# Layer 1's last five groups of tiles as routed pairs instead of dense experts

## The chip, the cores and the metric

The kernel runs on one core of one Trainium2 chip. Its metric is the device time of one execution in microseconds, the median of several runs. The engines are named as in the profile: PE multiplies matrices (PEld loads its weights), DVE works on vectors, ACT on activations and copies, POOL issues the indirect DMAs, and SP issues nearly all the others. Each engine takes its instructions in order, so one that waits holds up everything behind it on that engine.

## The reference

The input `x` has 8192 rows (128 graphs of 64 nodes) of 256 channels in fp32. Two layers follow each other. Each is a graph part over dense 64 x 64 adjacencies, added to `x`, and then a mixture-of-experts FFN over the rows, added to `x` again. The change is in the FFN of layer 1. It has four experts, of which every row uses two:

```python
h = (x_flat @ W_gat).reshape(M, HEADS, NUM_EXPERTS)          # M = B*N nodes of the graph, 4 heads
...   # attention over 1048576 random edges of 65536 nodes gives agg
scores = _layernorm(agg, ln_gamma, ln_beta).reshape(M, HEADS, NUM_EXPERTS).mean(1)
topk_s, topk_i = jax.lax.top_k(scores, TOP_K)                # TOP_K = 2
w = jax.nn.softmax(topk_s, axis=-1)
for ei in range(NUM_EXPERTS):
    g = jnp.where(topk_i == ei, w, 0.0).sum(-1)
    hh = jax.nn.gelu(x @ W1[ei] + b1[ei], approximate=False)  # 256 -> 512
    out = out + g[..., None] * (hh @ W2[ei] + b2[ei])         # 512 -> 256
```

The FFN of layer 1 is fed the layer-normed rows `z` (8192 of them). The weights of a row's two experts (its gates) depend on the attention over the edges and are known late; the outputs of the four experts depend on `z` alone.

## The kernel before

The 8192 rows are 64 tiles of 128 rows (`NT`), in 16 groups of `GR` = 4 tiles (`NG`). `x` stays in SBUF. Layer 0 ends at about 1200 us. In layer 1 there are four stages, and the dense expert work is dealt out over three of them, because it needs no gate to begin.

**The experts of one group** are the generator `experts` (L1025). For each of the four experts it issues four steps `h` (two 128x512 matmuls `ph` at L1035, the gelu at L1039) and four steps `y` (four 128x256 matmuls `py` at L1045, the bias add `y` on DVE at L1049, then `take`). It yields after each of these 32 units, so that the caller can put other work between them. The transposed rows `zT` of a group are loaded from the DRAM copy `zts` by `prepare`, one group ahead. What `take` does depends on the stage. Where the gates are unknown, `keep` stores the output tile to `ystore` (128 KB a time); with gates known, `add` (L1739) does `x += gate * y` on DVE (L1740) and sends the finished tile out (L1742).

**Beside stage, to 1687.5 us.** The graph part of layer 1 goes over the groups in steps: `first`, `second`, `combine`, `tables`. `combine` ends a group's `x`; `tables` (L1198) scales its rows to `z`, transposes them, stores them to `zts`, and makes the edge tables. `filler` (L1233) mixes into these steps the dense units of the first `BESIDE` = 4 groups; its outputs have names `p`, `pw` and `yin`. At the end of the stage the fillers that are left run out.

**Edge stage, to 2202.9 us.** It does the attention over the edges. `prologue` sets up sums, `edges_of_lists` (L1470) then makes 144 indirect gathers on POOL (`got`, L1485), selections on DVE and small matmuls. One of their steps is taken after each dense unit of groups 4 to 10 (`range(BESIDE, EARLY)`). 7 groups are 224 units. At its end is a branch on `n_trips`, the number of blocks of edges that didn't fit the lists; it isn't taken with these inputs.

**Gate stage and the rest.** `gates` (L1652) makes the gates of all 64 tiles, spread over the `y` units of group 11 (`EARLY`), whose outputs are kept too. Groups 12 to 15 then run with `add`. After each second unit the loads and adds of one of the 48 kept tiles are issued: `yin` from `ystore` (512 KB, pool `f2`, 3 buffers), four adds, one output store.

The buffers around the change: PSUM has 4 in the pool `psf`, which `ph` and `py` take from; outputs `y` have 6, gelu outputs `hT` 8.

Of the kernel before, what the change touches and what calls it, by code (L numbers as in the profile page):

```python
# [9 lines left out]
F32 = mybir.dt.float32  # L10
I32 = mybir.dt.int32
# [9 lines left out]
P = 128  # L21
NT = 64
# [41 lines left out]
PL = 24  # L64
NPC = 3
RK = 8
BESIDE = 4
EARLY = BESIDE + 7
HK = 8


# [5 lines left out]
def kernel(  # L77
# [52 lines left out]
        return t  # L130

    const = ctx.enter_context(tc.tile_pool(name="const", bufs=1, reuse_waits="tile"))
    small = ctx.enter_context(tc.tile_pool(name="small", bufs=2, reuse_waits="tile"))


    x = const.tile([P, NT, D], F32, name="x")
# [6 lines left out]
    V.memset(ones_col, 1.0)  # L143
    ones_row = const.tile([1, P], F32, name="ones_row")
    V.memset(ones_row, 1.0)

    def rsqrt(dst, v):

        V.tensor_copy(dst, v)
        s = small.tile([P, NT], F32, name="rs_s")  # L150
        S.activation(s, dst, AF.Sqrt)
        y = small.tile([P, NT], F32, name="rs_y")
        V.reciprocal(y, s)
        w = small.tile([P, NT], F32, name="rs_w")
        V.tensor_tensor(w, y, y, ALU.mult)
        V.tensor_tensor(w, w, dst, ALU.mult)
        V.tensor_scalar(w, w, -0.5, 1.5, ALU.mult, ALU.add)
        V.tensor_tensor(dst, y, w, ALU.mult)

    def root_of_bits(dst, v, guess, work):  # L160

# [847 lines left out]
    def scaled(dst, src, g, norm, k):  # L1009
        scale, shift, mean = factors(g, norm, k)  # L1010
        if norm == 0:
            S.activation(dst, src, AF.Identity, bias=shift, scale=scale)
        else:
            V.tensor_scalar(dst, src, mean, scale, ALU.subtract, ALU.mult)

    zts = dram.tile([NG, P, 2 * GR * P], F32, name="zts")
    ystore = dram.tile([EARLY + 1, GR, P, NEXP * D], F32, name="ystore")
    zTs = {}

    def prepare(g, to):  # L1020
# [3 lines left out]

    def experts(g, to, take, ahead=True):  # L1025

        if ahead and g + 1 < NG:
            prepare(g + 1, to)
        zT = zTs.pop(g)
        for e in range(NEXP):  # L1030
            hTs = []
            for q in range(NH1):
                ph = to["ph"]()
                for c in range(2):
                    nc.tensor.matmul(  # L1035
                        ph, w1[:, e, c, q * P : q * P + P], zT[:, c, :], start=(c == 0), stop=(c == 1)
                    )
                hT = to["hT"]()
                S.activation(hT, ph, AF.Gelu, bias=b1[:, e, q : q + 1])  # L1039
                hTs.append(hT)  # L1040
                yield "h"
            for k in range(GR):
                py = to["py"]()
                for q in range(NH1):
                    nc.tensor.matmul(  # L1045
                        py, hTs[q][:, k * P : k * P + P], w2[:, e, q, :], start=(q == 0), stop=(q == NH1 - 1)
                    )
                y = to["y"]()
                V.tensor_tensor(y, py, b2[:, e * D : e * D + D], ALU.add)  # L1049
                take(e, k, y)  # L1050
                yield "y"
# [7 lines left out]
    with ExitStack() as of_c:  # L1059
# [39 lines left out]
        def transposed(g, norm):  # L1099

            z = cz.tile([P, GR, D], F32, name="z")
            for k in range(GR):
                scaled(z[:, k, :], x[:, GR * g + k, :], g, norm, k)
            yield
            zT = c2.tile([P, 2, GR * P], F32, name="zT")
            for c in range(2):
                tz = psc.tile([P, GR * P], F32, name="tz")
                for k in range(GR):
                    nc.tensor.transpose(tz[:, k * P : k * P + P], z[:, k, c * P : c * P + P], ident)
                S.copy(zT[:, c, :], tz)  # L1110
            return zT
# [85 lines left out]

        def tables(g):  # L1198
            zT = yield from transposed(g, 2)
            nc.sync.dma_start(zts[g], zT.rearrange("p c n -> p (c n)"))  # L1200
            yield
            hps = psc.tile([P, D + 1], F32, name="ph")
            for k in range(GR):
# [353 lines left out]
    with tc.tile_pool(name="em", bufs=2, reuse_waits="tile") as emp, tc.tile_pool(name="pse", bufs=4, space=PSUM, reuse_waits="tile") as pse, tc.tile_pool(  # L1557
# [12 lines left out]
        V.tensor_reduce(some[0:1, :], trips[0:1, 0:P], AX.X, ALU.max)  # L1570
        V.tensor_scalar(n_trips, some[0:1, :], float(n_left), None, ALU.mult)
        n_trips = nc.values_load(n_trips[0:1, 0:1], min_val=0, max_val=n_left)
        for g in range(BESIDE, EARLY):
            for unit in experts(g, to, keep(g)):
                if not over:
                    over = next(steps, 1) == 1
                else:
                    next(edge_steps, None)
        for _ in edge_steps:
            pass  # L1580

# [59 lines left out]
    with tc.tile_pool(name="gp", bufs=1, reuse_waits="tile") as gp, tc.tile_pool(name="f2", bufs=3, reuse_waits="tile") as f2, tc.tile_pool(  # L1641
        name="psf", bufs=4, space=PSUM
    ) as psf:
        def by_channel(v):
            return v.unsqueeze(2).to_broadcast([P, HC, NT])

        def by_node(v, n):
            return v.unsqueeze(1).to_broadcast([P, n, NT])

        gate = gp.tile([P, NEXP, NT], F32, name="gate")  # L1650

        def gates():  # L1652

            agg = gp.tile([P, HC, NT], F32, name="agg")
            V.reciprocal(acc[:, 0:HEADS, :], acc[:, 0:HEADS, :])
            yield
            V.tensor_tensor(
                agg.rearrange("p (h c) t -> p h c t", c=NEXP),  # L1660
                acc[:, HEADS:CH, :].rearrange("p (h c) t -> p h c t", c=NEXP),
                acc[:, 0:HEADS, :].unsqueeze(2).to_broadcast([P, HEADS, NEXP, NT]),
                ALU.mult,
            )
            yield

            V.tensor_tensor(agg, agg, by_channel(bgat), ALU.add)
            yield
            m = gp.tile([P, NT], F32, name="m")
            V.tensor_reduce(m, agg.rearrange("p a t -> p t a"), AX.X, ALU.add)  # L1670
            yield
            V.tensor_scalar(m, m, 1.0 / HC, None, ALU.mult)
            yield
            V.tensor_tensor(agg, agg, by_node(m, HC), ALU.subtract)
            yield
            sq = gp.tile([P, HC, NT], F32, name="sq")
            V.tensor_tensor(sq, agg, agg, ALU.mult)
            yield
            V.tensor_reduce(m, sq.rearrange("p a t -> p t a"), AX.X, ALU.add)
            yield  # L1680
            V.tensor_scalar(m, m, 1.0 / HC, EPS, ALU.mult, ALU.add)
            yield
            rs = gp.tile([P, NT], F32, name="rs")
            rsqrt(rs, m)
            yield
            V.tensor_tensor(agg, agg, by_node(rs, HC), ALU.mult)
            yield
# [1 line left out]
            yield  # L1689
            V.tensor_tensor(agg, agg, by_channel(lnb), ALU.add)  # L1690
            yield
            sc = gp.tile([P, NEXP, NT], F32, name="sc")
            V.tensor_reduce(sc, agg.rearrange("p (h c) t -> p c t h", c=NEXP), AX.X, ALU.add)  # L1693
            yield
            V.tensor_scalar(sc, sc, 1.0 / HEADS, None, ALU.mult)
            yield

            rank = gp.tile([P, NEXP, NT], F32, name="rank")
            V.memset(rank, 0.0)
            yield  # L1700
            for e in range(NEXP):
                for f in range(e + 1, NEXP):
                    ge = f2.tile([P, NT], F32, name="ge")
                    V.tensor_tensor(ge, sc[:, e, :], sc[:, f, :], ALU.is_ge)  # L1704
                    yield
                    V.tensor_tensor(rank[:, f, :], rank[:, f, :], ge, ALU.add)  # L1706
                    yield
                    V.tensor_scalar(ge, ge, -1.0, 1.0, ALU.mult, ALU.add)  # L1708
                    yield
                    V.tensor_tensor(rank[:, e, :], rank[:, e, :], ge, ALU.add)  # L1710
                    yield
            V.tensor_reduce(m, sc.rearrange("p e t -> p t e"), AX.X, ALU.max)
            yield
            V.tensor_tensor(gate, sc, by_node(m, NEXP), ALU.subtract)
            yield
            S.activation(gate, gate, AF.Exp)
            yield
            V.tensor_scalar(rank, rank, 1.5, None, ALU.is_lt)
            yield
            V.tensor_tensor(gate, gate, rank, ALU.mult)  # L1720
            yield
            V.tensor_reduce(m, gate.rearrange("p e t -> p t e"), AX.X, ALU.add)  # L1722
            yield
            V.reciprocal(m, m)  # L1724
            yield
            V.tensor_tensor(gate, gate, by_node(m, NEXP), ALU.mult)
            yield

        steps = gates()

        to = places(psf, psf)
        for unit in experts(EARLY, to, keep(EARLY)):
            if unit == "y":
                for _ in range(4):
                    next(steps, None)
        for _ in steps:
            pass

# [2 lines left out]
            if e == NEXP - 1:  # L1741
                nc.sync.dma_start(out_t[:, t, :], x[:, t, :])  # L1742

        kept = iter([(g, k) for g in range(EARLY + 1) for k in range(GR)])
        for g in range(EARLY + 1, NG):
            n = 0
            for unit in experts(g, to, lambda e, k, y: add(GR * g + k, e, y)):
                n += 1
                if n % 2 == 0:
                    g0, k = next(kept, (None, None))  # L1750
                    if g0 is not None:
                        y = f2.tile([P, NEXP * D], F32, name="yin")
                        nc.sync.dma_start(y, ystore[g0, k])
                        for e in range(NEXP):
                            add(GR * g0 + k, e, y[:, e * D : e * D + D])


# [54 lines left out]
```

## Time and profile before

| | us |
|---|---|
| runs: lowest, median, highest | 2498.76, 2503.37, 2503.64 |
| profiled execution, own time | 2489.01 |
| its span, first to last instruction | 2487.3 |
| beside stage ends; edge stage ends | 1687.5; 2202.9 |
| busy PE, DVE, ACT, POOL (share of the span) | 91%, 63%, 37%, 12% |

The page gives busy times, slices of a fortieth of the span (62.2 us each), and groups of instructions with their mean duration. Matmuls are pipelined, so durations of matmuls are also read as the distance of their starts. The granted TensorE clock has a mean of 0.962. The stages' limits are read from the trace by the first and last instruction of each stage's lines.

### The profile page before, as it was taken

The page shows a single profiled execution, that of the slowest core. Times are in us where ns is not written, and L with a number is a line of the kernel's source. Part 1 is how long each engine was busy: PE and PEld are TensorE (multiplying, and loading weights), DVE is VectorE, ACT ScalarE, POOL GpSimd, SP SyncE. Part 2 cuts the span into 40 slices and gives each one's busy share as a digit, 9 for nine tenths or more (in the row PEclk, how much of TensorE's full clock was granted, in tenths as well). Part 3 has the DMA queues.
Part 4 walks back from the last instruction along what each step waited for, and adds up shares of the span by engine and source line. Part 5 has one row for each costly group of instructions (what it writes and reads, how often), then busy time and mean ns, then how long its engine had stood idle before and what let it go on. Part 6 is the DMA issues. An engine that isn't in the chain of part 4 may idle for free. (4 is left out here: it accounts for less than half of the span.)

```text
span 2487.3 us, 30612 instructions
## 1 busy us (share of the span) xinstructions
PE 2260.3 (91%) x10334; PEld 1441.9 (58%) x10334; DVE 1577.0 (63%) x4448; ACT 931.6 (37%) x1607; POOL 303.8 (12%) x331
## 2 busy tenths in 40 slices
PE   6889998897999999999487999998999999999999
PEld 4444444334566566566355676665676666666666
DVE  7989888317888888883388644615555552157822
ACT  3767666652211211211166757322333232121121
POOL 2011111111000000000331100002344341000000
PEclk9999999998999999999788999999999999999999
DMA  7121112302111121112214111122222121128800
GB/s 212 42 62 45 58 50 77 109 21 71 35 52 45 37 52 45 35 49 64 66 49 134 54 61 46 68 70 47 53 58 50 45 53 45 47 74 264 253 21 15
DMA packets 159204, 170.13 MB, mean 68 GB/s; under 512 B 43312, under 2 KB 137136, under 8 KB 159040
## 3 DMA queue, kind: packets, MB, share of 16 engines
q1 hardware_dynamic: 130848, 145.84, 19.3%
q0 software_dynamic: 10912, 18.31, 3.0%
q10 hardware_dynamic: 17280, 3.93, 0.7%
q8 instruction: 86, 1.41, 0.2%
q14 instruction: 78, 0.64, 0.1%
HBM read 100.42 MB, written 67.60 MB: 68 GB/s over the span
## 5 line engine op out<-in xcount | busy, mean ns | idle before, releaser
L476 PE MATMUL ph<-zT,w 128*128 128x512 f32 x1056 | 528.5, 633 | 32.3 <-ACT hT L479 19.7
L1045 PE MATMUL py<-w,hT 128*128 128x256 f32 x1536 | 362.3, 390 | 21.2 <-ACT hT L1039 12.5
L1035 PE MATMUL ph<-zT,w 128*128 128x512 f32 x768 | 348.3, 600 | 4.6 <-issue 4.2
L1045 PEld LDWEIGHTS py<-w,hT 128*128 128x128 f32 x1536 | 292.4, 194 | 85.8 <-issue 20.4
L476 PEld LDWEIGHTS ph<-zT,w 128*128 128x128 f32 x1056 | 196.7, 200 | 240.6 <-issue 178.7
L479 ACT ACTIVATE hT<-ph,b 128x512 f32<-128x512 f32 x264 | 179.9, 685 | 267.0 <-PE ph L476 264.3
L1039 ACT ACTIVATE hT<-ph,b 128x512 f32<-128x512 f32 x192 | 129.8, 687 | 364.9 <-PE ph L1035 361.6
L305 DVE TENSOR_TENSOR one<-iota_l,pb 128x1024 bf16<-128x1024 bf16 x208 | 253.4, 1218 | 18.0 <-PE cnt_ps L316 18.0
L903 PE MATMUL py<-wd,hT 128*128 x1088 | 250.1, 384 | 0.0
L1049 DVE TENSOR_TENSOR y<-py,b 128x256 f32<-128x256 f32 x192 | 80.8, 422 | 249.4 <-PE py L1045 244.2
L1035 PEld LDWEIGHTS ph<-zT,w 128*128 128x128 f32 x768 | 143.7, 191 | 154.5 <-issue 151.7
L903 PEld LDWEIGHTS py<-wd,hT 128*128 128x128 f32 x1088 | 202.1, 190 | 26.3 <-issue 1.4
L1485 POOL DMA_INDIRECT got<-tsrc,esrc x144 | 153.2, 1064 | 339.3 <-DVE lt L1461 149.7
L1089 POOL DMA_INDIRECT yin<-yrows,row_y x64 | 63.8, 997 | 764.3 <-SPq L966 632.1
L305 DVE TENSOR_TENSOR one<-iota_h,pb 128x512 bf16<-128x512 bf16 x208 | 141.8, 684 | 0.0
L467 ACT COPY zT<-tz 128x256 f32<-128x256 f32 x68 | 23.8, 374 | 291.1 <-PE tz L466 291.1
L622 PE MATMUL pre<-wd 128*128 128x512 f32 x256 | 127.3, 614 | 1.6 <-DVE x L647 0.9
L316 PEld LDWEIGHTS <-one 128*128 128x128 bf16 x1664 | 74.7, 98 | 84.1 <-issue 60.4
L1045 PE MATMUL pw<-w,hT 128*128 128x256 f32 x512 | 118.8, 380 | 0.0
L1035 PE MATMUL p<-zT,w 128*128 128x512 f32 x256 | 117.2, 600 | 1.8 <-ACT hT L1039 1.6
L1045 PEld LDWEIGHTS pw<-w,hT 128*128 128x128 f32 x512 | 94.9, 190 | 18.6 <-issue 6.7
L1740 DVE SCALAR_TENSOR_TENSOR x<-yin,gate,x 128x256 f32<-128x256 f32 x192 | 89.7, 481 | 23.3 <-DMA yin<-ystore 20.1
(369 smaller groups left out, 2999.8 us busy)
## 6 DMA issues: line engine op xcount, KB each, us to landing
yin<-ystore SPq DMA_DIRECT2D x48, 512.0 KB
ystore<-y SPq DMA_DIRECT2D x128, 128.0 KB
zin<-zrows SPq DMA_DIRECT2D x68, 128.0 KB
bd<-in_L_ffn_bd_dram SPq DMA_DIRECT2D x68, 128.0 KB
yrows<-y SPq DMA_DIRECT2D x68, 128.0 KB
x<-in_x_dram SPq DMA_DIRECT2D x8, 1024.0 KB
wd<-in_L_ffn_Wd_dram SPq DMA_DIRECT2D x8, 1024.0 KB
zts<-zT SPq DMA_DIRECT2D x16, 512.0 KB
```

Source lines behind the costliest of these rows:

```text
L305: V.tensor_tensor(o, wi.unsqueeze(1).to_broadcast([P, HK, n]), pb[:, g : g + HK].unsqueeze(2).to_broadcast([P, HK, n]), ALU.is_equal,)
L316: nc.tensor.matmul(self.ps, one[0][:, k, :], one[1][:, k, :], start=(at + k == 0), stop=(at + k == n_chunks * KEPT - 1),)
L476: nc.tensor.matmul(ph, w1[:, c, q * P : q * P + P], zT[:, c, :], start=(c == 0), stop=(c == 1))
L479: S.activation(hT, ph, AF.Gelu, bias=b1[:, q : q + 1])
L622: nc.tensor.matmul(pre, xnT[:, c, n * P : n * P + P], wcat[:, c, :], start=(c == 0), stop=(c == 1),)
L903: nc.tensor.matmul(py, hTs[q][:, k * P : k * P + P], wd[:, bass.ds(ex[k], 1), q, :].rearrange("p e f -> p (e f)"), start=(q == 0), stop=(q ...
L1035: nc.tensor.matmul(ph, w1[:, e, c, q * P : q * P + P], zT[:, c, :], start=(c == 0), stop=(c == 1))
L1039: S.activation(hT, ph, AF.Gelu, bias=b1[:, e, q : q + 1])
L1045: nc.tensor.matmul(py, hTs[q][:, k * P : k * P + P], w2[:, e, q, :], start=(q == 0), stop=(q == NH1 - 1))
L1049: V.tensor_tensor(y, py, b2[:, e * D : e * D + D], ALU.add)
L1485: nc.gpsimd.indirect_dma_start(got, None, tsrc, bass.IndirectOffsetOnAxis(ap=esrc[:, b, at : at + 1], axis=0))
L1740: V.scalar_tensor_tensor(x[:, t, :], y, gate[:, e, t : t + 1], x[:, t, :], ALU.mult, ALU.add)
```

## The change

Layer 1's last five groups (20 tiles of 128 rows, tiles 44 to 63) are no longer computed for all four experts. The other 11 groups (`DENSE`) stay dense. Their distribution is new: 2 groups as fillers (before 4), 5 in the edge stage (before 7), 2 in the gate stage (before 1), and 2 at the very end (before 4).

- **In the tables**, the rows `z` of the routed groups are stored to `zns`, and no `zts` for them.
- **At the start of the edge stage**, 23 DMAs of 256 KB fill the DRAM array `zslots` with zeros. A tile of it has the 128 slots of some rows of one expert. Two steps of the edge work are taken per dense unit before the gathers and behind them, one while they run.
- **In the gate stage**, two steps per unit of groups 7 and 8: gates of the 20 routed tiles first, then `route`, then gates of the other 44. `gates` is written with fewer yields, and its reciprocal square root is made on DVE by `root_of_bits` instead of with ACT's square root. `route` counts by small matmuls how many rows come before each row in its expert, and gives every row two slots (`place`), rounded up to pairs of tiles per expert: 23 pairs at most (`PAIRS`). It loads the `z` rows of five groups (into the `f2` buffers of `yin`) and sends each tile twice to `zslots`, by 40 indirect DMAs on POOL. `pair_e` holds the expert of each pair.
- **`pairs`** goes over the 23 pairs with the expert's number in registers of SP and PE. Each loads its slots, the expert's `w1` (512 KB), `b1` and `b2` from DRAM, transposes, and does the two layers with 128x256 matmuls (`w2` from SBUF at a dynamic place), and stores its two tiles to `yslots`. After each sixth unit a kept tile may be taken.
- **`back`**, beside the dense groups 9 and 10: for each routed tile, two indirect gathers from `yslots`, two adds with `weight`, and its output store.

The diff, cut to its core (the steps of the gates that only lose a yield, and a few lines of set-up, are left out):

```diff
-BESIDE = 4
-EARLY = BESIDE + 7
+BESIDE, EDGES, GATES = 2, 7, 9
+ROUTED = 5
+DENSE = NG - ROUTED
+RT = ROUTED * GR
+PAIRS = RT + 3
...
+            if norm == 2 and g >= DENSE:
+                nc.sync.dma_start(zns[g - DENSE], z.rearrange("p k f -> p (k f)"))
...
-            nc.sync.dma_start(zts[g], zT.rearrange("p c n -> p (c n)"))
+            if g < DENSE:
+                nc.sync.dma_start(zts[g], zT.rearrange("p c n -> p (c n)"))
...
-        for g in range(BESIDE, EARLY):
+        none = e1.tile([P, D], F32, name="none")
+        nc.gpsimd.memset(none, 0.0)
+        for i in range(PAIRS):
+            nc.sync.dma_start(
+                zslots[2 * P * i : 2 * P * i + 2 * P].rearrange("(k p) f -> p k f", p=P),
+                none.unsqueeze(1).to_broadcast([P, 2, D]),
+            )
+        taken = 0
+        for g in range(BESIDE, EDGES):
             for unit in experts(g, to, keep(g)):
-                if not over:
-                    over = next(steps, 1) == 1
-                else:
-                    next(edge_steps, None)
+                for _ in range(1 if over and taken < ET * NB else 2):
+                    if not over:
+                        over = next(steps, 1) == 1
+                    else:
+                        next(edge_steps, None)
+                        taken += 1
...
+        def route():
...
+            for k in range(ROUTED):
+                z = f2.tile([P, NEXP * D], F32, name="yin").rearrange("p (k f) -> p k f", f=D)
+                nc.sync.dma_start(z.rearrange("p k f -> p (k f)"), zns[k])
+                for i in range(GR):
+                    for j in range(2):
+                        t = k * GR + i
+                        send = nc.gpsimd.indirect_dma_start(
+                            zslots, bass.IndirectOffsetOnAxis(ap=place[:, j, t : t + 1], axis=0), z[:, i, :], None
+                        )
+                        for other in sends:
+                            tc.declare_no_dep(send.ins, other, reason="no two write the same row")
+                        sends.append(send.ins)
...
-        for unit in experts(EARLY, to, keep(EARLY)):
-            if unit == "y":
-                for _ in range(4):
-                    next(steps, None)
+        steps = chain(gates(T0, NT), route(), gates(0, T0))
+        for g in range(EDGES, GATES):
+            for unit in experts(g, to, keep(g)):
+                next(steps, None)
+                next(steps, None)
...
+        def kept():
+            for t in range(GATES * GR):
+                y = f2.tile([P, NEXP * D], F32, name="yin")
+                nc.sync.dma_start(y, ystore[t // GR, t % GR])
+                for e in range(NEXP):
+                    add(t, e, y[:, e * D : e * D + D])
+                yield
+
+        def pairs():
+            for i in range(PAIRS):
...
+                e = bass.ds(ex[i % GR], 1)
+                z = fp.tile([P, 2, D], F32, name="zin")
+                nc.sync.dma_start(z, zslots[2 * P * i : 2 * P * i + 2 * P].rearrange("(k p) f -> p k f", p=P))
+                w1e = fp.tile([P, 2, F1], F32, name="w1e")
+                nc.sync.dma_start(w1e, f1_w1[e].rearrange("e (c p) f -> p (e c) f", p=P))
...
+                b2e = fp.tile([P, D], F32, name="b2e")
+                nc.sync.dma_start(b2e, f1_b2[e, :].to_broadcast([P, D]))
+                tz = to["ph"]()
+                for c in range(2):
+                    for k in range(2):
+                        at = (2 * c + k) * P
+                        nc.tensor.transpose(tz[:, at : at + P], z[:, k, c * P : c * P + P], ident)
+                zT = fp.tile([P, 2, 2 * P], F32, name="zTp")
+                S.copy(zT.rearrange("p c n -> p (c n)"), tz)
+                yield
+                hTs = []
+                for q in range(NH1):
+                    ph = to["ph"]()[:, 0 : 2 * P]
...
+                for k in range(2):
+                    py = to["py"]()
...
+                    y = to["y"]()
+                    V.tensor_tensor(y, py, b2e, ALU.add)
+                    nc.sync.dma_start(yslots[(2 * i + k) * P : (2 * i + k + 1) * P, :], y)
+                    yield
+
+        def back():
+            for t in range(RT):
+                ys = []
+                for j in range(2):
+                    y = fb.tile([P, D], F32, name=f"yb{j}")
+                    nc.gpsimd.indirect_dma_start(
+                        y, None, yslots, bass.IndirectOffsetOnAxis(ap=place[:, j, t : t + 1], axis=0)
+                    )
+                    ys.append(y)
+                    yield
+                xs = x[:, T0 + t, :]
+                for j in range(2):
+                    V.scalar_tensor_tensor(xs, ys[j], weight[:, j, t : t + 1], xs, ALU.mult, ALU.add)
+                nc.sync.dma_start(out_t[:, T0 + t, :], xs)
+
+        stored = kept()
+        with tc.tile_pool(name="fp", bufs=2, reuse_waits="tile") as fp:
+            for n, _ in enumerate(pairs()):
+                if n % 6 == 5:
+                    next(stored, None)
+        with tc.tile_pool(name="fb", bufs=3, reuse_waits="tile") as fb:
+            steps = back()
+            for g in range(GATES, DENSE):
+                for n, _ in enumerate(experts(g, to, lambda e, k, y: add(GR * g + k, e, y))):
+                    next(steps, None)
+                    if n % 3 == 2:
+                        next(stored, None)
+            for of in (stored, steps):
+                for _ in of:
+                    pass
```

The tiles are scheduled by the framework, which may issue an instruction ahead of others that stand before it in the code; the order named in the prediction is that of the engines' built instruction streams.

## The prediction

> **What bounds the kernel now.** I read the page's sums and slices first, to see which engine is full and when; then a table of windows, cut where one stage ends; then the groups of instructions in the stages that the change touches; last the chain that ended last, which is matmuls alone from 2351.8 us on. The page:
>
> ```profile
> PE 2260.3 (91%) x10334; PEld 1441.9 (58%) x10334; DVE 1577.0 (63%) x4448; ACT 931.6 (37%) x1607; POOL 303.8 (12%) x331
> ...
> PE   6889998897999999999487999998999999999999
> ...
> DVE  7989888317888888883388644615555552157822
> ```
>
> PE has nine tenths or more in all slices from 1366 us on but one, so what the change takes from PE there is time, unless something else is late. The windows (columns: length; busy PE, PEld, DVE, ACT, POOL with counts; granted clock; DMA share; GB/s):
>
> ```profile
> 1366.00:1560.00 194.00, 190.97 (x877) 134.17 (x876) 106.52 (x348) 128.34 (x208) 8.40 (x8) 1.00 0.16 52
> 1560.00:1600.00 40.00, 40.00 (x177) 28.18 (x176) 35.63 (x150) 15.49 (x24) 0.33 (x2) 1.00 0.26 88
> 1600.00:1640.00 40.00, 40.00 (x172) 28.27 (x172) 4.89 (x14) 8.80 (x14) 0.00 (x0) 1.00 0.21 73
> 1640.00:1688.00 48.00, 47.81 (x187) 33.01 (x186) 7.82 (x21) 9.32 (x14) 0.00 (x0) 1.00 0.19 61
> 1688.00:1720.00 32.00, 31.11 (x128) 19.94 (x129) 25.49 (x67) 9.04 (x12) 1.12 (x2) 1.00 0.26 42
> 1720.00:1800.00 80.00, 70.27 (x350) 47.65 (x349) 39.96 (x96) 24.49 (x61) 36.89 (x35) 0.91 0.22 48
> 1800.00:2060.00 260.00, 250.34 (x1343) 176.53 (x1341) 141.17 (x363) 83.37 (x190) 114.07 (x107) 0.98 0.21 51
> 2202.00:2300.00 98.00, 97.11 (x327) 63.17 (x328) 79.35 (x183) 26.13 (x35) 0.00 (x0) 0.97 0.61 195
> ```
>
> From 1560 to 1688 DVE is nearly done by 1600, and PE works on fillers alone. The edge stage (1687.5 to 2202.9) and the gate stage with the groups behind it (to 2487.3) are full of the same dense expert work. Its groups between 2202 and 2400 us (busy, mean ns of one | idle before):
>
> ```profile
> L1035 PE MATMUL ph<-zT,w 128*128 128x512 f32 x224 | 101.2, 606 | 4.2 <-issue 4.2
> L1045 PE MATMUL py<-w,hT 128*128 128x256 f32 x447 | 99.3, 380 | 1.1 <-DVE y L1049 1.1
> L1740 DVE SCALAR_TENSOR_TENSOR x<-yin,gate,x 128x256 f32<-128x256 f32 x192 | 89.7, 481 | 23.3 <-DMA yin<-ystore 20.1
> ```
>
> The records are pipelined; start to start, a 128x512 matmul takes 0.853 us here and a 128x256 one 0.433. One expert of a group is 8 x 0.853 + 16 x 0.433 = 13.8 us, a group of four tiles 55.1. The third row is the 48 kept tiles: DVE and their loads run beside PE, 48 in 128 us, 2.67 us each, a load landing 4.4 us (median) after its issue. On POOL, from the page, one indirect DMA is:
>
> ```profile
> L1485 POOL DMA_INDIRECT got<-tsrc,esrc x144 | 153.2, 1064 | 339.3 <-DVE lt L1461 149.7
> L1089 POOL DMA_INDIRECT yin<-yrows,row_y x64 | 63.8, 997 | 764.3 <-SPq L966 632.1
> ```
>
> Issued back to back they start 1.28 us apart.
>
> **The change, part by part.** All times are of the profiled execution: span 2487.3, own time 2489.0. That is 14 us (0.6%) under the median of the runs, 2503.4; I add the same 14 us at the end. About 0.2%, 5 us, is what a measurement of this kernel tells from no change.
>
> *Fillers 4 to 2 groups.* Up to 1560 nothing differs. From there groups 2 and 3 are missing: 110.3 us of PE work. But DVE has 35.6 of 40 us until 1600, and the last factors come at 1599; the four last tables follow each other at filler pace (1600, 1620, 1640, 1660) only because fillers lie between them, and need 9 us of PE in all. So the stage ends at about 1602 (1598 to 1612) instead of 1687.5: 85 of the 110 us are gained, 25 are work that was free.
>
> *Edge stage, 7 to 5 groups.* 514.9 less two groups, 404.6 us, if the edge steps are still spread over the units. They are: two steps a unit in the prologue and after the 144th gather, so 160 units suffice; one step a unit between keeps the gathers at their present pace. New there: 23 zero fills of 256 KB, 16 of them on SP's queue ahead of the prologue's loads: 16 x 0.4 us of issue, and 5.9 MB at the 253 to 264 GB/s of the fullest slices is 23 us of transfers; the first gather comes 31 us after the stage's start and PE has units to do, so I put 2 on it (0 to 17). Each of the five routed groups' z rows is stored where zT was, 512 KB for 512 KB: even. Gate stage starts at 1602 + 405 + 2 = 2009 (2000 to 2030), 194 earlier.
>
> *Gates and routing, beside groups 7 and 8.* PE has 2 x 55.1 = 110.3 us of work and three small matmul groups of routing. The gate chain for 20 tiles and the routing go in two steps a unit of 1.72 us: about 38 steps, 33 us until the places are known (25 to 40; the 64-tile chain of before takes 30 at two to four steps a unit; one ACT table load of L151, 1.28 us, goes). Then 40 sends x 1.28 = 51 us on POOL, last landing 87 us in (no indirect send stands in this stage of the trace; the first layer's, L750, and L1485 are the nearest rows: 40 x 1.0 at the least, 40 x 1.3 at the most). Behind them SP's queue is in order: the five z loads share the three kept-tile buffers, so the fourth waits for send 8, the fifth for 16, the first kept tile for 24. Stores of groups 7 and 8 are queued behind those loads; six y buffers fill, and PE stands some 18 us, later 6. The scheduler has put 24 kept loads on SP and 106 kept adds (26 tiles) on DVE ahead of what the first pair needs: pair 0's weights and its bias add. Most of these tiles come after 87 us, at 2.67 us each (lower end 4 adds x 0.48 = 1.95 us; upper end 3.3, if the 4.4 us landing is covered by two buffers only). 87 + 22 x 2.67 = 146, and the first weights, 512 KB loads that landed in 5.5 to 9.7 us when they were first loaded, with four transposes make 156 (140 to 172). PE's 110 us leave 42 of idle time: the moved kept tiles, cheap beside dense groups, are on the path here.
>
> *Pairs for 5 dense groups.* A pair of slots: 4 transposes 0.44, the wait for ACT's copy of 128x512 (0.58, with hand-overs 1.0), 8 + 8 matmuls of 128x256 = 6.94: 8.4 us. 23 of them 193 us, and 4 for six loads of expert numbers into PE's registers (0.6 us each, as the one for n_trips); the 5 groups were 275.7. Saved: 79. The bias adds, gelus and 46 stores of 128 KB lie beside PE: DVE has 2 x 0.42 and ten kept tiles 19 us in 193. Loads of one pair are 0.9 MB, two buffers deep, so they have about 8 us to land; at 195 GB/s, as in the gate stage now, they need 4.6. Hidden; without cover each us counts 23 times.
>
> *Last two groups and the gathers back.* 110.3 us. The 40 gathers need every pair's store and then run at 1.28 us; 32 of them are queued, with their adds, on DVE ahead of the second expert's first bias adds in group 9. They take 41 us plus 3 of landing, PE has some 28 us until it needs those adds: a stall of 15 (8 to 22). Tail as now, 4.
>
> *Clock.* After PE idles the granted clock falls: 0.91 over 80 us in the row from 1720 is 14 us at half rate, 7 lost after one such gap. Four stalls of 6 to 42 us here; I take 8 us for all (4 to 20).
>
> The Trainium skill ("TensorE: Matmul & The Clock Gate", Part 1) has the array at half clock after one idle window of about 3.4 us, until one busy window has passed. By that rule four stalls would cost 4 x 1.7 = 7 us, an estimate; the row says 7 for one, and the sum would be up to 20 higher by it.
>
> Sum: 2009 + 156 + 197 + 110 + 15 + 4 + 8 = 2499 span, 2501 own time, 12 over 2489: **2515 us** on the scale of the median. As a balance: PE's work falls by 79; against it stand 25 us of lost cover, 42 + 15 + 8 of standing and some 6 of zeros and routing, less 5 that the gate stage stood before.
>
> **The rivals.**
> *PE work alone decides (faster).* If kept tiles, sends and gathers hide, the 42, 15 and most of the 8 us are gone: 2515 - 60 = 2455. For it: PE is bound by work everywhere now, and L1740 hides today. Against: 22 kept tiles x 2.67 us cannot lie beside the 23 us of PE work that are left 87 us in. It wins over the forecast if the kept tiles start before the sends finish. Chance 0.20, band 2440 to 2478.
> *A pair waits for its own loads (slower).* Zeros, 512 KB of weights and a broadcast bias land later than 8 us after their issue: the bias broadcast bd of the first layer took 3.9, but first weight loads of 512 KB took 5.5 to 9.7 us. At 10.5 us a pair: 23 x 2.1 = 48 more, 2563. It decides from a landing of 8.4 us on. Against: the DMA share in these stretches is 0.2. Chance 0.18.
> *The stage before does not shrink (slower).* Tables stay 10 to 20 us apart without fillers because their own chain (scale, transpose, copy, matmul, copy, store) is that long: 40 us more, 2555. For: all of it is serial; against: four tables have 13 us of DVE work between 1600 and 1688. Chance 0.07.
>
> **How the numbers follow.** The forecast's case has 0.55, with its own range 2488 to 2540; in it 0.11 is faster, 0.12 within 0.2%, 0.32 slower. Faster 0.20 + 0.11 = 0.31, same 0.12, slower 0.32 + 0.18 + 0.07 = 0.57. For 8 in 10 I leave out the lower half of the first rival (0.10) and the upper half of the second (0.09): 2460 to 2563.
>
> **What would show it.** Right: PE idle from 1560 on with the edge stage at about 1602; gate stage at about 2009; ph of the first pair some 156 us later, waiting on kept adds or its weights; pairs 8.4 us apart, waiting on ACT's zTp; a PE wait in group 9 for DVE. Wrong: pairs further apart than 9 us with DMA as releaser (second rival); no PE gap over 10 us before the pairs (first rival); the edge stage after 1620 (third).

## The result and the profile after

The changed kernel takes 2533.99 us (median of 4 runs, 2530.37 to 2544.07) where the kernel before takes 2503.51 (4 runs): 1.013 of it, 95% interval 1.0096 to 1.0163, 30 us slower. The profiled execution took 2534.8 us, span 2533.1. In the page, busy times and slices (40 of 63.3 us):

```profile
PE 2193.6 (87%) x10206; PEld 1428.8 (56%) x10206; DVE 1556.9 (61%) x4458; ACT 937.8 (37%) x1644; POOL 375.3 (15%) x421
...
PE   6889988897999999999388998789998985799969
...
PEclk9999999997999999999688999699999997899989
```

PE has 67 us less to do than before and stands 87% busy instead of 91%. Where it stands is seen in the slices: 8 7 8 from 1520 to 1710 us, with a clock of 0.6 in the second of them; 8 5 7 from 2026 to 2216 us, in the gate stage; and the 6 from 2406 us on. The windows cut at the stages (length; busy PE, PEld, DVE, ACT, POOL; granted clock; DMA share; GB/s):

```profile
1560.00:1600.00 40.00, 26.00 (x121) 20.60 (x121) 32.30 (x120) 12.24 (x21) 0.64 (x3) 0.68 0.25 85
1600.00:1620.00 20.00, 16.96 (x67) 13.89 (x67) 10.11 (x64) 2.15 (x4) 0.00 (x0) 0.50 0.44 145
2033.00:2100.00 67.00, 53.37 (x168) 32.00 (x168) 38.44 (x148) 16.43 (x21) 24.61 (x26) 0.88 0.31 106
2100.00:2183.00 83.00, 64.66 (x224) 43.77 (x224) 45.40 (x103) 12.39 (x19) 14.31 (x15) 0.86 0.76 243
2183.00:2392.00 209.00, 178.74 (x829) 151.78 (x830) 46.53 (x108) 56.99 (x115) 0.00 (x0) 0.96 0.57 175
2392.00:2450.00 58.00, 34.63 (x108) 21.28 (x107) 24.26 (x56) 5.17 (x8) 38.34 (x40) 0.83 0.47 134
```

Who ended PE's idle time from 2033 us on (us in total, times, longest):

```profile
PE py L1040 <- ACT hT L1034: 47.2, 5, 13.1
PE ph L1899 <- ACT zTp L1893: 16.0, 22, 0.7
PE ph L1899 <- DMA w1e<-in_L_ffn_W_dram: 14.3, 1, 14.3
PE py L1040 <- issue: 7.7, 1, 7.7
```

The first row is put down to ACT, which was not short of time: it had 16, 12 and 5 us of work in the windows from 2033, 2100 and 2392 us. 22.5 of its 47.2 us, and the 7.7, lie between 2086 and 2120 us, beside the sends; 24.7 lie at 2411 and 2440, beside the gathers. PE waits there for gelus that start late. The chain that ended last has them like this beside the sends (start, length, what; the last four gelus are those of one expert):

```profile
2072.86 1.26 ACT hT L1034 x2
2074.13 13.69 another core or an unknown queue
2087.90 0.69 ACT hT L1034
2088.59 7.68 another core or an unknown queue
2096.35 0.69 ACT hT L1034
2097.03 11.13 another core or an unknown queue
2108.25 0.69 ACT hT L1034
2108.93 9.76 issue
2118.76 0.69 ACT hT L1034
```

The matmuls `ph` of these four gelus ran from 2079.0 to 2086.1 us. Besides them a gelu needs only ACT itself and an `hT` buffer that earlier `py` matmuls have read, and each of the four starts 7 to 11 us after the last of these was ready. The two late gelus beside the gathers, at 2423 and 2451 us, start 17.5 and 16.0 us after it. No instruction of DVE, SP or POOL lies between, and the profile doesn't name what released them. In the kernel before, no gelu from the edge stage on starts more than 1.5 us late.

DVE stood as well between 2033 and 2200 us, with one wait of 20.3 us for the first kept tile:

```profile
DVE x L1854 <- DMA yin<-ystore: 42.9, 13, 20.3
```

The stages beside the forecast, by the first instruction of their lines:

| | forecast | measured |
|---|---|---|
| edge stage begins | 1602 | 1617.4 |
| gate stage begins | 2009 | 2033.2 |
| first pair's `ph`, after that | 156 | 164.1 |
| 23 pairs | 197 | 192.8 |
| last two groups to the end | 137 | 143.0 |
| span | 2499 | 2533.1 |

### The profile page after: what moved, and what is told of

Its sections match the earlier page's. It is cut to its first block, busy times and chain, and to the rows that moved or that the text cites. A ratio compares the mean times of both kernels' runs of the same rounds, so it can differ in the third digit from the quotient of the medians.

```text
span 2533.1 us, 31135 instructions
## 1 busy us (share of the span) xinstructions
PE 2193.6 (87%) x10206; PEld 1428.8 (56%) x10206; DVE 1556.9 (61%) x4458; ACT 937.8 (37%) x1644; POOL 375.3 (15%) x421
## 5 line engine op out<-in xcount | busy, mean ns | idle before, releaser
L467 PE MATMUL ph<-zT,w 128*128 128x512 f32 x1056 | 530.1, 635 | 30.4 <-ACT hT L470 17.8
L1040 PE MATMUL py<-w,hT 128*128 128x256 f32 x1152 | 284.6, 401 | 71.7 <-ACT hT L1034 53.9
L467 PEld LDWEIGHTS ph<-zT,w 128*128 128x128 f32 x1056 | 196.6, 200 | 239.2 <-issue 179.6
L1040 PEld LDWEIGHTS py<-w,hT 128*128 128x128 f32 x1152 | 224.8, 200 | 127.4 <-ACT hT L1034 62.3
L470 ACT ACTIVATE hT<-ph,b 128x512 f32<-128x512 f32 x264 | 180.0, 685 | 266.9 <-PE ph L467 264.0
L1030 PE MATMUL ph<-zT,w 128*128 128x512 f32 x576 | 268.4, 609 | 4.8 <-issue 4.8
L1034 ACT ACTIVATE hT<-ph,b 128x512 f32<-128x512 f32 x144 | 96.0, 686 | 303.8 <-PE ph L1030 206.3
L1030 PEld LDWEIGHTS ph<-zT,w 128*128 128x128 f32 x576 | 107.8, 193 | 112.6 <-issue 110.8
L1044 DVE TENSOR_TENSOR y<-py,b 128x256 f32<-128x256 f32 x144 | 59.9, 421 | 148.6 <-PE py L1040 122.8
L1854 DVE SCALAR_TENSOR_TENSOR x<-yin,gate,x 128x256 f32<-128x256 f32 x144 | 68.4, 483 | 77.3 <-DMA yin<-ystore 74.3
L1899 PE MATMUL ph<-zTp,w1e 128*128 128x256 f32 x368 | 88.0, 393 | 30.3 <-ACT zTp L1893 16.0
L741 POOL DMA_INDIRECT zrows<-z,pos x64 | 64.0, 1001 | 292.0 <-issue 75.2
L902 DVE TENSOR_TENSOR y<-py,bd 128x256 f32<-128x256 f32 x68 | 28.8, 423 | 117.5 <-PE py L894 114.9
```

The lines of the kernel that those rows point to most:

```text
L467: nc.tensor.matmul(ph, w1[:, c, q * P : q * P + P], zT[:, c, :], start=(c == 0), stop=(c == 1))
L470: S.activation(hT, ph, AF.Gelu, bias=b1[:, q : q + 1])
L1030: nc.tensor.matmul(ph, w1[:, e, c, q * P : q * P + P], zT[:, c, :], start=(c == 0), stop=(c == 1))
L1040: nc.tensor.matmul(py, hTs[q][:, k * P : k * P + P], w2[:, e, q, :], start=(q == 0), stop=(q == NH1 - 1))
L1854: V.scalar_tensor_tensor(x[:, t, :], y, gate[:, e, t : t + 1], x[:, t, :], ALU.mult, ALU.add)
L1899: nc.tensor.matmul(ph, w1e[:, c, q * P : q * P + P], zT[:, c, :], start=(c == 0), stop=(c == 1),)
```

## The experiments

All ratios are to the kernel before on the same chip at the same time; it took 2466 to 2506 us there, so times of different sets don't compare. The first nine versions ran on chip 7 (before: 2494 to 2506 us), those with five buffers on chips 12 and 4 (2467 and 2466); the record names no chip for the result. A difference to the changed kernel is that of the two ratios, 0.001 being 2.5 us. The profiles are compared by stage.

**Fillers alone.** The kernel before with `BESIDE = 2`:

```diff
-BESIDE = 4
+BESIDE = 2
```

> The kernel before with one number changed: fillers of 2 groups instead of 4 beside the graph part, so 7 groups beside the edges, 1 beside the gates, 6 at the end; all four experts of all tiles, no routing. Theory (lost cover): the beside stage ends 70 to 85 us earlier and the end gets 110 us more, so 25 to 40 us slower than the kernel before, about 2535; PE idles after 1560 us and its granted clock falls to about 0.7 there. Rival (the fillers cost the stage nothing that matters, the changed kernel loses its time behind it): within 8 us of the kernel before. A second question: the edge stage of the changed kernel began at 1617 us, where 1602 had been worked out. If the zero fills held it up, it begins at 1602 to 1606 here, where there are none; if the clock after PE's gaps did, at 1608 to 1615.

Measured: 1.0155 (1.0125 to 1.0185), 36 us. The moved fillers alone make the kernel as slow as the whole change does; on top of them routing changed the time by some 6 us, within the intervals. In its windows PE is idle and slow at the same place:

```profile
1560.00:1600.00 40.00, 25.38 (x116) 19.89 (x114) 30.60 (x123) 10.63 (x17) 0.33 (x2) 0.60 0.23 77
1600.00:1611.00 11.00, 8.74 (x39) 8.25 (x39) 4.72 (x33) 1.68 (x4) 0.00 (x0) 0.50 0.27 98
```

Its edge stage begins 244.2 us after the first filler, and so does the changed kernel's (1617.4 - 1373.2). So the zero fills, which this version doesn't have, don't delay the start of the stage; PE's two gaps of 5 us and the half clock behind them are what the forecast's 236 us left out. The gaps in the changed kernel (in us: total, times, longest; this version has them as long):

```profile
PE tz L1106 <- DVE z L1005: 9.3, 6, 5.0
PE tz L1106 <- DVE mf L154: 5.2, 1, 5.2
```

**Kept tiles behind the pairs' loads.** On the changed kernel, `loads` holds the last load of each pair:

```diff
-                nc.sync.dma_start(y, ystore[t // GR, t % GR])
+                with tc.issue_after(loads[-1]):
+                    nc.sync.dma_start(y, ystore[t // GR, t % GR])
```

> The changed kernel, but each kept tile's load is issued on SP's queue behind the loads of the pair it was written beside, so no kept tile lies ahead of the first pair; all work stays. Theory (queue order): the first pair's matmuls start 30 to 45 us earlier in the gate stage, near 125 us after its start instead of 164, pairs stay at 8.4 us, and some kept tiles move into the last dense groups: 25 to 40 us faster than the changed kernel, 2495 to 2509. Rival (the sends and transfers hold the pairs): the 40 sends end where they ended and the first pair's slots and weights land no earlier, so less than 10 us faster; or the pairs stretch to 9.5 us and more because a 512 KB kept load lies between their own loads, which gives 25 us back.

Measured: 1.0281 (1.024 to 1.0322), 38 us slower than the changed kernel. The first pair came 16 us earlier (148.0), but a pair took 10.41 us instead of 8.38, 47 us in all. Between 2170 and 2420 us PE waited for weights that stood behind a kept tile:

```profile
PE ph L1902 <- DMA w1e<-in_L_ffn_W_dram: 38.4, 13, 5.5
PE ph L1902 <- ACT zTp L1896: 7.2, 10, 0.7
```

The rival's second half held. It is also the forecast's slow rival (10.5 us a pair, 48 us), brought about by hand: its price was right, and the changed kernel escapes it because 26 of its 36 kept tiles lie ahead of the first pair's weights. One thing more is seen here: no kept tile lies ahead of the pairs, DVE waits for none before the first pair, and PE still stands 25 us beside the sends, for gelus that start 5 to 10 us late.

**Three groups beside the gates.**

```diff
-BESIDE, EDGES, GATES = 2, 7, 9
+BESIDE, EDGES, GATES = 2, 7, 10
```

> The changed kernel with three dense groups beside the gates and the sends, and one behind the pairs (two and two in the change); the same work in all. Theory (PE stands because 44 us of kept tiles and weights are ahead of the pairs): the third group fills that gap, and behind the pairs the stall for the gathered rows' adds stays at about 25 us: 30 to 45 us faster than the changed kernel, 2490 to 2505. Rival (the gap is made of stores and y buffers behind the sends, not of a lack of work): the gap before the pairs stays over 30 us, and the time within 10 us of the changed kernel. Another loss that could show: 40 gathers of 1.28 us need 51 us, one group gives 55, so the end may get 5 to 15 us longer.

Measured: 1.0098 (1.0066 to 1.013), 8 us faster than the changed kernel; the theory wanted 30 to 45. The end got 56 us shorter (87.0) and the first pair came 47 us later (211.2). The wait for the weights shrank from 14.3 to 5.8 us, but PE's waits beside the sends were still 24 us (30 in the changed kernel). More work behind the stall does not fill it.

**Gathered adds behind the bias adds.** `bias_adds` takes the dense groups' L1044:

```diff
+                    with tc.issue_after(bias_adds[-1]):
                         V.scalar_tensor_tensor(xs, ys[j], weight[:, j, t : t + 1], xs, ALU.mult, ALU.add)
```

> The changed kernel, but each gathered tile's two adds stand on DVE behind the dense bias add that they were written after, instead of up to 32 of them ahead of the bias adds of group 9; nothing else moves. Theory (queue order): the two waits of PE in group 9 (13.1 and 11.6 us in the profile) go, and the half clock behind them: 20 to 30 us faster than the changed kernel, 2504 to 2514. Rival (PE waits there for the y or gather buffers, or for POOL): the wait moves to the next unit, under 8 us faster.

Measured: 1.0018 (1.0001 to 1.0034), 28 us faster than the changed kernel. The end takes 118.6 us instead of 143.0. Of the wait for `hT` in it this is left:

```profile
PE py L1042 <- ACT hT L1036: 1.8, 2, 1.4
```

The stall goes with the adds' place on DVE, whatever engine the row named. But the edit also spreads the gathers, whose buffers are free later (62 us from the first to the last instead of 53), so on this chip it doesn't tell the order of adds from whatever held the gelus. The version with five buffers, further down, has the old order of adds and no late gelu; at its end PE waits 12.6 us, for DVE:

```profile
PE py L1040 <- DVE y L1044: 12.6, 3, 11.6
```

**No wait for sends on SP.** The `z` loads and the slots' loads are issued on POOL:

```diff
-                nc.sync.dma_start(z.rearrange("p k f -> p (k f)"), zns[k])
+                nc.gpsimd.dma_start(z.rearrange("p k f -> p (k f)"), zns[k])
...
-                nc.sync.dma_start(z, zslots[2 * P * i : 2 * P * i + 2 * P].rearrange("(k p) f -> p k f", p=P))
+                nc.gpsimd.dma_start(z, zslots[2 * P * i : 2 * P * i + 2 * P].rearrange("(k p) f -> p k f", p=P))
```

> The changed kernel, but the five z loads and the 23 loads of slots, which wait for sends, are issued on POOL's queue behind the sends, not on SP's in front of the stores of groups 7 and 8. Theory (SP stands behind the sends, y buffers fill, PE waits): the four waits of PE between 53 and 87 us after the gate stage's start (30 us with half clock behind them) go, and the dense groups end 30 to 35 us earlier. The kept tiles then decide the first pair, 2.7 us each, and keep some of it back: 10 to 30 us faster than the changed kernel (1.013 of the kernel before), 1.001 to 1.009. Rival (PE waits there for DVE, which does the gates, or for the sends' traffic): the waits stay, within 5 us of the changed kernel.

Measured: 1.0089 (1.0062 to 1.0115), at the slow end of the theory's range, and its interval overlaps the changed kernel's. In the profile the first pair comes at 163.0 us, as before: PE's waits beside the sends shrank from 30 to 21 us and the wait for weights grew from 14 to 19. The end takes 152.1 us instead of 143.0. The theory, that the four waits go, was wrong. DVE still stood for the kept tiles, whose buffers the sent rows held:

```profile
DVE x L1854 <- DMA yin<-ystore: 57.5, 17, 18.2
```

**Three fillers.**

```diff
-BESIDE, EDGES, GATES = 2, 7, 9
+BESIDE, EDGES, GATES = 3, 8, 10
```

> The changed kernel with the 11 dense groups dealt out 3, 5, 2, 1 instead of 2, 5, 2, 2: a third filler group beside the graph part, one group less behind the pairs. Theory (lost cover; 36 us between two and four fillers without routing): the beside stage ends 20 to 28 us later, with no PE gap of 5 us near 1575 us, the end gets 55 us less: 25 to 35 us faster than the changed kernel, less what the 40 gathers (51 us) lose of their cover, 5 to 10 us: 0.999 to 1.006 of the kernel before. Rival (the graph part's own chain had room for two fillers only): the beside stage ends 50 us later and nothing is won, 1.011 to 1.015.

Measured: 0.9939 (0.9919 to 0.9958), better than the theory's range. By stage, the edge stage begins 269.0 us after the first filler instead of 244.2, and the end takes 88.2 instead of 143.0: 30 of the 48 us. 9 more lie in the edge stage (407 us instead of 416), which has the same work. The same 40 us as above, now with PE full at the full clock:

```profile
1560.00:1600.00 40.00, 39.83 (x176) 28.70 (x176) 35.07 (x130) 15.33 (x26) 0.64 (x3) 1.00 0.32 112
```

**Three edits.** The last three together:

> The two edits above together with the later adds of the gathered tiles (28 us faster by itself): three fillers, nothing that waits for sends on SP, gathered adds behind the bias adds. If the three losses are separate, they add: 1.002 less 15 to 25 us for SP and 20 to 30 for the filler, 0.980 to 0.988 of the kernel before, the first version that is faster than it. If they share a cause (PE's idle time moves on to the next wait), 0.995 or more.

Measured: 0.9884 (0.9864 to 0.9903), just outside the range. They add up to 61 us of the 86 that they gave one by one: with one group at the end instead of two, later adds save 12 us of it (76.0 against 88.2) instead of 24.

**Own buffers for the sent rows**, two of 128 KB, on top of the waits off SP:

```diff
-                z = f2.tile([P, NEXP * D], F32, name="yin").rearrange("p (k f) -> p k f", f=D)
-                nc.gpsimd.dma_start(z.rearrange("p k f -> p (k f)"), zns[k])
                 for i in range(GR):
+                    zi = fz.tile([P, D], F32, name="zr")      # pool fz has 2 buffers
+                    nc.gpsimd.dma_start(zi, zns[k, :, i * D : i * D + D])
```

> The changed kernel with the waits for sends off SP as before (1.0089), and the sent rows in two 128 KB buffers of their own, one tile at a time, instead of in the three buffers of the kept tiles. Theory (kept tiles stand in front: on DVE their adds are queued ahead of the bias adds of groups 7 and 8, and they can't have a buffer before the sends are through): kept tiles start some 45 us after the gate stage's start, DVE no longer stands, PE's idle time before the first pair falls from 44 us to 10 to 20 and the first pair's matmuls start 125 to 140 us after the stage's start instead of 162: 20 to 35 us faster than with the waits off SP alone, 0.995 to 1.001 of the kernel before. Rival (SP's or DVE's gates, not the kept tiles, hold PE): the first pair stays at 155 us or later, 1.006 or more. The two small buffers could slow the sends from 51 to 75 us, which the theory's range contains.

Measured: 1.011 (1.0091 to 1.013): no gain in time. But PE's waits beside the sends are gone but for 3.4 us, and so are the late gelus there; the two dense groups end 120 us after the stage's start instead of 149. Then PE stands 30.6 us for the first slots, because now the sends are slow: 109 us from the first to the last instead of 50, waiting for their two buffers. The first pair comes at 152.4 us, 12 earlier, and the end gives 11 back (153.7 us), with a gelu that starts 25 us late. So the run doesn't tell the free buffers from the slower sends as what ended the waits. PE's row, and then POOL's from the groups:

```profile
PE ph L1891 <- DMA zin<-zslots: 30.6, 1, 30.6
```

```profile
L1812 POOL DMA_DIRECT2D zr<-zns x18 | 10.3, 574 | 35.3 <-DMA zslots<-zr,place 33.8 <-issue 1.6
```

**The same with three fillers and later adds:**

> The same with the two edits that paid before: three fillers (3, 5, 2, 1) and the gathered tiles' adds behind the bias adds (0.9884 with the waits off SP, without own buffers). Theory: the first pair 125 to 140 us after the gate stage's start instead of 160.6, the rest as in that kernel: 20 to 35 us less, 0.975 to 0.981 of the kernel before. Rival: PE's time is by then bound by its own work and the gain is under 8 us, 0.985 or more.

Measured: 0.9843 (0.9822 to 0.9863), between the two: the first pair at 153.1, for the same reason.

**Five buffers of 512 KB**, in the room where the pairs' buffers lie later; slots' loads on POOL, `z` loads on SP as in the change:

```diff
-                z = f2.tile([P, NEXP * D], F32, name="yin").rearrange("p (k f) -> p k f", f=D)
+                z = fz.tile([P, NEXP * D], F32, name="zr").rearrange("p (k f) -> p k f", f=D)
...
+        with tc.tile_pool(name="fz", bufs=ROUTED, reuse_waits="tile") as fz:
+            for g in range(EDGES, GATES):
...
```

> The changed kernel with five 512 KB buffers of their own for the sent rows (in the room that the pairs' buffers take later), all five loads ahead of the sends, and the slots' loads on POOL. Nothing on SP or DVE waits for a send, and no send waits for a buffer. With two small buffers the sends took 110 us instead of 50 and PE, which had run its two groups without a wait in 119 us, stood 31 us for them. Theory (the stall has two parts, kept work queued ahead and the sends): sends end 84 to 90 us after the gate stage's start, the dense groups at 115 to 120, the first pair's matmuls at 120 to 130 instead of 164: 30 to 40 us faster than the changed kernel, 0.997 to 1.002 of the kernel before. Rival (32 kept tiles on SP ahead of the first pair's weights are then the last): 135 us or later, 1.004 or more.

Measured: 0.9929 (0.9908 to 0.995), more than the theory's range gave. The last send starts at 86.7 us (84.4 in the changed kernel), the dense groups end at 120, and the first pair is at 138.3: 26 us earlier than in the changed kernel, but in the rival's range. No gelu starts more than 0.4 us late. This is the first version on another chip, and the changed kernel itself didn't run there: the edge stage, which the edit doesn't touch, takes 384 us instead of 416. What of the 26 us is the buffers' and what the chip's is not shown. What PE waits for then is the third thing in the queue, the weights behind 31 kept tiles:

```profile
PE ph L1900 <- DMA w1e<-in_L_ffn_W_dram: 18.3, 1, 18.3
```

**The same with three fillers and later adds:**

> The same with three fillers (3, 5, 2, 1) and the gathered tiles' adds behind the bias adds. Theory: 25 to 30 us less than with the two small buffers (0.9843), 0.972 to 0.976 of the kernel before. Rival (what is taken before the pairs comes back behind them, as the last group has only 55 us to cover 40 gathers of 1.28 us): 0.980 or more, with PE waiting in the last group.

Measured: 0.9754 (0.973 to 0.9778), as the theory said, on chip 12 too.

**Weights sooner.** On that version:

```diff
-                nc.sync.dma_start(y, ystore[t // GR, t % GR])
+                with tc.issue_after(loads[0]) if t >= 22 else ExitStack():
+                    nc.sync.dma_start(y, ystore[t // GR, t % GR])
```

> The best version so far (0.9754) with one edit: of the kept tiles, 22 instead of 32 stand ahead of the first pair's weights on SP; the others are queued behind them, beside the first eleven pairs. Theory (the 18.1 us that PE still waits for w1e are kept tiles in front of it, 2.7 us each): the wait falls under 5 us and the kept tiles hide beside the pairs as ten did before: 10 to 16 us faster, 0.969 to 0.972. Rival (a kept tile's 512 KB between the pairs' own loads stretches them, as when all 36 lay there and pairs took 10.4 us): pairs of 9 us and more, nothing gained, 0.975 or more.

Measured: 0.971 (0.969 to 0.973), 2397.67 us against 2466.28 of the kernel before. The first pair is at 122.4 us instead of 140.8, and both mechanisms show: the wait for weights is 4 us at the first pair, but three more come later, and a pair takes 8.75 us instead of 8.39 (8 us in 23):

```profile
PE ph L1905 <- ACT zTp L1899: 13.8, 19, 0.7
PE ph L1905 <- DMA w1e<-in_L_ffn_W_dram: 11.5, 4, 4.1
```

## Why the prediction was right, and where it was not

The direction, the balance (79 us of PE work against lost cover and standing time) and the range held: 2534 us lies in 2460 to 2563, and slower had 0.57. The steps:

- **What bounds it** held, and so did the cost of a pair: 8.38 us against 8.4. 8.38 is 192.8 / 23; from the second pair on, the pairs stand 8.34 us apart, every one of them, so the 4 us for register loads were not seen. PE saves 275.7 - 192.8 = 83 us.
- **Fillers**: named rightly, sized too small. The stage ended 244 us after the first filler and not 236. The forecast priced the missing fillers as cover alone, and left the half clock of a PE that idles in gaps of 5 us out of this stage: clock 0.68 over 40 us and then 0.50 over 20, when it does the last tables. With three fillers it is 1.00 there. The rule that the forecast took from the Trainium skill ("TensorE: Matmul & The Clock Gate", Part 1, half clock after about 3.4 us of idleness) agrees with the gaps of 5.0 and 5.2 us, which end at 1577 and 1589 us. The other 7 us of the stage's 15 were there at the first filler already (1373.2 against 1366.0), before anything that the change alters there; the profiles of the experiments have 1367 to 1377 at this place on chip 7, and 1354 to 1359 on the other two.
- **First pair at 156 us**: 164 measured, and PE's standing time was 44 us as forecast 42. That the two agree is in part luck, because the forecast's parts are not what the runs show. It let SP's waits stop PE for 24 us, and 22 kept tiles behind the sends set the end. In the trace PE stands 30 us for gelus that start late, and no instruction of SP or DVE lies between these and their input. SP's waits taken away left 21 of the 30 us, and the kept tiles taken away left 25. Only the versions with own buffers for the sent rows have none of it: two with sends 2.8 us apart on chip 7, the others on chips 12 and 4. So what held the gelus is open; that it is the shared buffers, or both queues at once, is not shown. The other 14 us are as forecast: the first pair's weights, behind kept tiles.
- **Gathers**: 24.7 us instead of 15. The forecast's reason, adds queued ahead on DVE, is seen alone in the version with five buffers, where it costs 12.6 us, near the forecast. In the changed kernel PE's two waits there are for gelus that start 17.5 and 16.0 us late, and what held these is open too. The end's 143 us less 110 of work and 24.7 of waits leave 8 for the clock and the tail, where the forecast had 12.
- **The rivals**: "PE work alone" did not happen: PE stood 44 us before the pairs and 24.7 behind them. With five send buffers, three fillers, later adds and sooner weights 0.971 comes out, on another chip, where that rival had 2455 us, 0.981. "A pair waits for its loads" did not happen, and was worth 47 us when it was made to. "The stage before does not shrink" did not happen.
- **The scale** failed: the profiled execution of before was 14 us under its median, and the forecast added those 14 us to its sum. The profiled execution of after is within 1 us of its median. The sum was 34 us short of the span it spoke of, 19 short on the median: the added 14 us hid nearly half of the miss.

Why the edge stage took 416 us and not 407 is open. With the same instructions in it, it took 403 to 416 us in the profiles on chip 7, and 384 in the one with five buffers on chip 12, where PE's waits for DVE's `y` there fell from 8.0 to 0.7 us. The three-filler versions have 405 to 407 us on chip 7 and 376 to 377 on chips 12 and 4. The kernel before is 27 to 40 us faster on these two as well.

## What to carry to other kernels

Work that is taken out of a stage where another engine sets the end is worth only what sticks out, and less when the engine that now idles drops its clock: moving one filler group back was worth 48 us here. A wait that the profile puts on one engine can be made elsewhere: look when that engine's own input was ready, and which instruction stands in front of it on its in-order queue. Where the input was long ready and nothing stands in front, as for the late gelus here, the order of the program is not yet the reason. For transfers that wait for a late event, try buffers and a queue of their own together: here moving only the queue left 21 of 30 us, own buffers with it left none, and too few of them moved the wait to the sends. Compare versions on one chip; a stage that no edit touched was 30 us shorter on another.

## What the runs showed of the hardware that was not expected

- An indirect send of 128 rows starts 1.3 us after the one before when five tiles' loads are ahead of it (51 us for 40), and 2.8 us after it (109 us for 40) when each tile must wait for one of two buffers: the landing of sends and loads is then in the loop.
- Gelus of the dense groups start late while POOL issues sends or gathers 1.25 to 1.28 us apart: by up to 11 us beside the sends of the changed kernel, and by up to 25 us beside the gathers of the version with two own buffers. Beside that version's sends, 2.8 us apart, none is over 1 us late, and on chips 12 and 4 none from the edge stage on is over 0.4 us late, with sends and gathers as close. Why is open.
- The kernel before took 2466 to 2506 us (medians) in the runs beside the experiments, a spread of 1.6% with no difference in the program: 2494, 2506 and 2499 on chip 7, 2467 on chip 12, 2466 on chip 4. The ratios' intervals are 0.2 to 0.4% to either side all the same.
